# Inverse roots of layer 1's norms by GpSimd's power operation instead of Newton steps on VectorE

## The chip, the cores and the metric

The kernel runs on one core of one Trainium2 chip. The metric is the device time of one execution in microseconds (us), median of several runs. Beside it stands the profile of one execution, whose span (first to last instruction) is 1.7 to 2.2 us shorter than the time of that same execution. A run counts as slow when it is over 1.5% above the fastest of the same kernel, and as fast otherwise. The ratios below use fast runs alone, and the traces are of fast runs unless it is said otherwise; a median from a slow chip can include slow runs. The runs fell on several chips; on some of them, called slow chips below, the unchanged kernel itself takes 565 us or more instead of 504, so each kernel is compared with the runs of the unchanged kernel made with it on the same chip, and the ratios that come of this are set beside one another only where the unchanged kernel took 503 to 506 us.

## The reference, cut to what matters

Two layers work on 2708 nodes of 128 features with a sparse adjacency matrix, each followed by a residual norm. The change touches only the two norms of layer 1:

```python
def _layernorm(x, axis=-1, eps=1e-5):
    m = jnp.mean(x, axis=axis, keepdims=True)
    v = jnp.var(x, axis=axis, keepdims=True)
    return (x - m) / jnp.sqrt(v + eps)

# layer 1, for every pair (i, j) with an edge: gelu(s[i] + d[j] + msg_b), summed with weight adj
new_feats = combined @ upd_w.T + upd_b
h = gelu(new_feats) + node_feats
mu, var = mean(h), var(h)                       # per row
l1 = (h - mu) / sqrt(var + LN_EPS) * ln_w + ln_b
x = _layernorm(x + l1)
```

So each row needs two inverse square roots, one per norm, with a product by `ln_w`, a sum with `ln_b` and a sum with `x` between the two norms.

## The kernel before

The 2708 rows are 22 blocks of 128, worked through in seven groups of 4, 4, 4, 4, 3, 2 and 1 blocks. For each group GpSimd gathers rows of a table (98 gathers in all), TensorE, VectorE and ScalarE turn them into messages and sums, and `finish` makes the two norms and stores the group.

```python
GROUPS = [(0, 4), (4, 4), (8, 4), (12, 4), (16, 3), (19, 2), (21, 1)]
for g0, gn in GROUPS:
    h = fin.tile([P, gn, D], F32, name="h")
    for b in range(g0, g0 + gn):
        ...                                     # cut
        for k0 in range(t0, t1, 4):
            dd = edge.tile([P, 4, D], F32, name="dd", bufs=4)
            ...                                 # cut: w gathers, matmuls, products
                gather(dd[:, k, :], table, J[:, t : t + 1])
    finish(h, g0, gn)

def rsqrt(o, v, shape):
    h = fin.tile([P, shape], I32, name="rh")
    t = fin.tile([P, shape], F32, name="rt")
    nc.vector.tensor_scalar(h, v.bitcast(I32), 1, None, op0=OP.arith_shift_right)
    nc.vector.tensor_scalar(o.bitcast(I32), h, -1.0, MAGIC, op0=OP.mult, op1=OP.add)
    for _ in range(3):
        nc.vector.tensor_mul(t, o, o)
        nc.vector.tensor_mul(t, t, v)
        nc.vector.tensor_scalar(t, t, -0.5, 1.5, op0=OP.mult, op1=OP.add)
        nc.vector.tensor_mul(o, o, t)

def layer_norm(o, v, n):
    ...                                         # cut: tiles st, mv, ve, rs
    for k in range(n):
        nc.vector.bn_stats(st[:, k, :], v[:, k, :])
        nc.vector.bn_aggr(mv[:, k, :], st[:, k, :])
    nc.vector.tensor_scalar_add(ve, mv[:, :, 1], LN_EPS)
    rsqrt(rs, ve, n)
    for k in range(n):
        nc.vector.tensor_scalar(o[:, k, :], v[:, k, :], mv[:, k, 0:1], rs[:, k : k + 1],
                                op0=OP.subtract, op1=OP.mult)

def finish(h, b0, n):
    own = x1[:, b0 : b0 + n, :]
    v = fin.tile([P, n, D], F32, name="v")
    nc.scalar.activation(h, h, AF.Gelu)
    nc.vector.tensor_add(h, h, own)
    layer_norm(v, h, n)
    nc.gpsimd.tensor_mul(v, v, rowvec["lw"]...)   # these three are called a trio below
    nc.gpsimd.tensor_add(v, v, rowvec["lb"]...)
    nc.gpsimd.tensor_add(v, v, own)
    layer_norm(h, v, n)
    ...                                         # cut: the stores of the group's rows
```

A root is thus 2 + 3 x 4 = 14 instructions on VectorE, on `n` numbers per partition.

Of the kernel before, what the change touches and what calls it, by code (L numbers as in the profile page):

```python
# [10 lines left out]
F32 = mybir.dt.float32  # L11
U32 = mybir.dt.uint32
BF16 = mybir.dt.bfloat16
I32 = mybir.dt.int32
AF = mybir.ActivationFunctionType
OP = mybir.AluOpType
AX = mybir.AxisListType

P = 128
# [4 lines left out]
MAGIC = 1597463007.0  # L24
# [26 lines left out]
def hyperbolic_then_message_kernel(  # L51
# [16 lines left out]
    nc = tc.nc  # L68
# [11 lines left out]
    const = ctx.enter_context(tc.tile_pool(name="const", bufs=1))  # L80
# [24 lines left out]
    for name, src in (("ub", upd_b), ("lw", ln_w), ("lb", ln_b), ("mbr", msg_b)):  # L105
        t = const.tile([P, D], F32, name=name)
# [3 lines left out]
    ones = const.tile([P, P], F32, name="ones")  # L110
    nc.gpsimd.memset(ones, 1.0)

    tri = const.tile([P, P], F32, name="tri")
    nc.gpsimd.affine_select(
        tri, ones, pattern=[[1, P]], compare_op=OP.is_gt, fill=0.0, base=0, channel_multiplier=-1
# [61 lines left out]
    def cols():  # L177
        count[0] += 1
        return sc.tile([P, NB], F32, name=f"c{count[0]}")
# [55 lines left out]
    def bank(name, bufs=2):  # L235
        return ps.tile([P, 512], F32, name=name, bufs=bufs)

    with tc.tile_pool(name="stream", bufs=2) as stream, tc.tile_pool(name="small", bufs=2) as small:
# [22 lines left out]
        u, v, gam, gm1 = cols(), cols(), cols(), cols()  # L261
# [85 lines left out]
        for b in range(NB):  # L347
# [8 lines left out]
            op = bank("mp")  # L356
# [72 lines left out]
    with tc.tile_pool(name="edge", bufs=2) as edge, tc.tile_pool(name="fin", bufs=2) as fin:  # L429
# [3 lines left out]

        def rsqrt(o, v, shape):

            h = fin.tile([P, shape], I32, name="rh")
            t = fin.tile([P, shape], F32, name="rt")
            nc.vector.tensor_scalar(h, v.bitcast(I32), 1, None, op0=OP.arith_shift_right)
            nc.vector.tensor_scalar(o.bitcast(I32), h, -1.0, MAGIC, op0=OP.mult, op1=OP.add)
            for _ in range(3):  # L440
                nc.vector.tensor_mul(t, o, o)
                nc.vector.tensor_mul(t, t, v)
                nc.vector.tensor_scalar(t, t, -0.5, 1.5, op0=OP.mult, op1=OP.add)
                nc.vector.tensor_mul(o, o, t)

        def layer_norm(o, v, n):
            st = fin.tile([P, n, 6], F32, name="st1")
            mv = fin.tile([P, n, 2], F32, name="mv1")
            ve = fin.tile([P, n], F32, name="ve1")
            rs = fin.tile([P, n], F32, name="rs1")  # L450
# [6 lines that stand above are left out]
                nc.vector.tensor_scalar(  # L457
                    o[:, k, :], v[:, k, :], mv[:, k, 0:1], rs[:, k : k + 1], op0=OP.subtract, op1=OP.mult
                )
# [24 lines left out]
# [3 lines that stand above are left out]
# [6 lines left out]
                for k0 in range(t0, t1, 4):  # L493
# [4 lines left out]
                    for k in range(w):  # L498
                        t = k0 + k
# [49 lines left out]
    with tc.If(dense > 0):  # L549
        with tc.tile_pool(name="dn", bufs=1) as fin:  # L550
# [17 lines left out]
            for b in range(NB):  # L568
                h = fin.tile([P, 1, D], F32, name="h")
# [63 lines left out]
```

## Time and profile before

| | before |
|---|---|
| time, median (lowest to highest) | 503.59 us (503.42 to 503.71) |
| span of the profiled run (its own time: 504.96 us) | 503.2 us |
| VectorE (DVE) busy | 315.3 us, 63% |
| GpSimd (POOL) busy | 227.9 us, 45% |
| first gather of layer 1's table | 312.75 us |
| 98th and last gather | 444.15 us |
| last VectorE instruction ends | 498.06 us |
| last GpSimd instruction ends | 494.27 us |

The page's section on the chain of work that ended last gives, for the kernel before, its shares of the span by engine:

```profile
PE 43%; DVE 22%; POOL 15%; issue 8%; ACT 7%; DMA 5%; POOLq 0%; ACTq 0%; DVEq 0%; SPq 0%
```

VectorE's 22% and GpSimd's 15% are what a change of this kind can move; TensorE's (PE) 43% belong mostly to layer 0. The strips, the gathers and the timelines that the argument rests on are shown in the prediction.

### The profile page before, as it was taken

Reading aid. Unit: us, or ns where it says so; the run is one execution under the profiler, and the core shown is the slowest. Engines: PE = TensorE matmul, PEld = TensorE weight load, DVE = VectorE, ACT = ScalarE, POOL = GpSimd, SP = SyncE. Lnnn points to the kernel's source line nnn. Section 1 sums busy time; section 2 is a strip of 40 time slices with the busy share of each in tenths; the row PEclk is TensorE's granted clock in tenths of the full one; section 3 lists DMA queues with packets and bytes.
Section 4 is the critical chain, followed back from the end, with each engine's and each line's share of the span. In section 5 each row is a group of like instructions: output and inputs, shape, how many; then the busy total and the mean of one; then the engine's idle time right before and its main releaser. Section 6 shows DMA issues by size and latency. Waiting matters only on the chain.

```text
span 503.2 us, 7459 instructions
## 1 busy us (share of the span) xinstructions
PE 320.8 (64%) x2506; PEld 297.9 (59%) x2506; DVE 315.3 (63%) x1161; ACT 158.2 (31%) x321; POOL 227.9 (45%) x306
## 2 busy tenths in 40 slices
PE   2682998999999999994000097576777094855200
PEld 1451997999999999993000065465666094844200
DVE  3539485777676676678989965222363184755774
ACT  2953143453644544532242045211121021211100
POOL 4200077777645544542000001777777878662211
PEclk9995897999999999998555579579899679686555
DMA  7500332455464564500000012121212121210000
GB/s 262 240 1 2 115 123 110 150 198 191 157 231 144 204 222 162 195 2 0 1 0 0 1 52 65 53 53 52 52 54 53 37 74 38 68 26 23 21 18 14
DMA packets 17719, 43.55 MB, mean 87 GB/s; under 512 B 6180, under 2 KB 12620, under 8 KB 14860
## 3 DMA queue, kind: packets, MB, share of 16 engines
q1 hardware_dynamic: 10108, 35.94, 19.7%
q0 software_dynamic: 6272, 6.49, 5.5%
q10 hardware_dynamic: 1296, 0.60, 0.5%
q8 instruction: 21, 0.34, 0.3%
q14 instruction: 22, 0.18, 0.1%
HBM read 40.18 MB, written 2.83 MB: 85 GB/s over the span
## 4 chain that ended last, share of the span: by engine, by line
PE 43%; DVE 22%; POOL 15%; issue 8%; ACT 7%; DMA 5%; POOLq 0%; ACTq 0%; DVEq 0%; SPq 0%
PE mp L358 21%; POOL dd L162 10%; PE sel L334 5%; PE kx L285 5%; DMA dd<-table_dram,J 3%; PE kx L418 3%; ACT sgn L351 2%; PE ag L511 2%; DVE c L196 2%; PE kx L248 2%; DMA x_sb<-in_x_dram 2%; POOL v L475 1%; POOL v L476 1%; POOL v L477 1%; PE kx L501 1%
## 5 line engine op out<-in xcount | busy, mean ns | idle before, releaser
L162 POOL DMA_INDIRECT dd<-table_dram,J x98 | 93.9, 958 | 96.9 <-DMA table_dram<-nom 66.4
L162 POOL DMA_INDIRECT V<-in_adj_dram,F x98 | 94.5, 965 | 93.3 <-DVE F L343 57.5
L358 PE MATMUL mp<-y,aT 128*128 128x130 f32 x968 | 134.1, 286 | 3.4 <-ACT sgn L351 3.4
L358 PEld LDWEIGHTS mp<-y,aT 128*128 128x128 f32 x968 | 120.0, 196 | 3.7 <-ACT sgn L351 3.7
L290 DVE MAX8 top<-kx 128x8 f32<-128x512 f32 (+4 forms) x179 | 85.6, 512 | 6.6 <-PE kx L285 6.3
L351 ACT ACTIVATE sgn<-aT 128x2816 bf16<-128x2816 f32 x22 | 56.1, 2552 | 67.0 <-PE kx L285 56.4
L285 PE MATMUL kx<-kd,sgn 128*128 128x128 bf16 x484 | 44.8, 225 | 9.5 <-DVE top L290 9.5
L502 PE MATMUL kx<-ident,R 128*128 128x128 f32 x98 | 27.0, 322 | 32.0 <-DVE dd L508 23.6
L501 PE MATMUL kx<-y,R 128*128 128x128 f32 x196 | 39.6, 315 | 7.1 <-DVE dd L508 6.3
L508 DVE TENSOR_TENSOR dd<-kx,dd 128x512 f32<-128x512 f32 (+3 forms) x30 | 17.7, 589 | 41.3 <-DMA dd<-table_dram,J 35.2
L285 PEld LDWEIGHTS <-sgn 128*128 128x128 bf16 x484 | 36.4, 103 | 11.8 <-DVE top L290 9.2
L509 ACT ACTIVATE ge<-dd 128x512 f32<-128x512 f32 (+3 forms) x30 | 16.6, 552 | 77.2 <-DVE dd L508 43.5
L511 PE MATMUL ag<-rw,ge 128*128 128x128 f32 x196 | 35.6, 334 | 7.4 <-ACT ge L509 3.2
L501 PEld LDWEIGHTS kx<-y,R 128*128 128x128 f32 x196 | 33.7, 228 | 8.8 <-DVE dd L508 7.7
L415 PE MATMUL mp<-ident,x_sb 128*128 128x128 f32 x22 | 5.1, 317 | 50.3 <-DVE x_sb L411 50.3
L511 PEld LDWEIGHTS ag<-rw,ge 128*128 128x128 f32 x196 | 31.5, 241 | 9.3 <-ACT ge L509 8.8
L502 PEld LDWEIGHTS kx<-ident,R 128*128 128x128 f32 x98 | 15.2, 167 | 34.3 <-DVE dd L508 25.4
L415 PEld LDWEIGHTS mp<-ident,x_sb 128*128 128x128 f32 x22 | 3.5, 161 | 52.0 <-DVE x_sb L411 50.5
L334 PE MATMUL sel<-z,R 128*128 128x49 f32 (+3 forms) x196 | 28.0, 288 | 7.3 <-DVE R L309 4.5
L334 PEld LDWEIGHTS sel<-z,R 128*128 128x128 f32 x196 | 25.3, 201 | 8.9 <-issue 5.0
L452 DVE BATCH_NORM_STATS2 st<-v 128x6 f32<-128x128 f32 x22 | 5.5, 275 | 37.1 <-POOL v L477 37.1
L319 DVE TENSOR_TENSOR_SCAN scan<-m,oe 128x48 f32<-128x48 f32 (+3 forms) x24 | 8.8, 368 | 30.1 <-ACT oe L303 30.0
(169 smaller groups left out, 539.2 us busy)
## 6 DMA issues: line engine op xcount, KB each, us to landing
aT<-in_adj_t_dram SPq DMA_DIRECT2D x22, 1408.0 KB
V<-in_adj_dram,F POOLq DMA_INDIRECT x98, 2.9
dd<-table_dram,J POOLq DMA_INDIRECT x98, 2.6
table_dram<-nom SPq DMA_DIRECT2D x22, 64.0 KB
out_dram<-h SPq DMA_DIRECT2D x21, 64.0 KB
mw<-in_L_gnn_msg_w_dram ACTq DMA_DIRECT2D x1, 128.0 KB
uw<-in_L_gnn_upd_w_dram ACTq DMA_DIRECT2D x1, 128.0 KB
w_sb<-in_L_gnn_W_dram ACTq DMA_DIRECT2D x1, 64.0 KB
```

The lines of the kernel that those rows point to most:

```text
L162: nc.gpsimd.indirect_dma_start(out=o, out_offset=None, in_=src, in_offset=bass.IndirectOffsetOnAxis(ap=at, axis=0))
L285: nc.tensor.matmul(kp[:, i * P : (i + 1) * P], lhsT=sgn[:, j, :], rhs=kd[:, j, :], start=True, stop=True)
L290: nc.vector.max(top[:, c : c + 8], seg[:, s, :])
L334: nc.tensor.matmul(sp[:, k, :], lhsT=R[:, t0 + k0 + k, :], rhs=z, start=True, stop=True)
L351: nc.scalar.activation(sgn, aT, AF.Sign, accum_out=signs[:, b : b + 1])
L358: nc.tensor.matmul(op[:, : D + 2], lhsT=aT[:, j, :], rhs=y[:, j, :], start=(j == 0), stop=(j == NB - 1))
L418: nc.tensor.matmul(dp[:, : 2 * D], lhsT=x1T[:, b * P : (b + 1) * P], rhs=wT[:, 0:2, :].rearrange("p a d -> p (a d)"), start=True, stop=True,)
L501: nc.tensor.matmul(X[:, k, :], lhsT=R[:, t, :], rhs=s_nm[:, b, :], start=True, stop=True)
L502: nc.tensor.transpose(RT[:, k, :], R[:, t, :], ident)
L508: nc.vector.tensor_tensor(dd[:, :w, :], X[:, :w, :], dd[:, :w, :], op=OP.add)
L509: nc.scalar.activation(ge[:, :w, :], dd[:, :w, :], AF.Gelu)
L511: nc.tensor.matmul(ag[:, :P], lhsT=ge[:, k, :], rhs=rw[:, k, :], start=False, stop=(k0 + k == t1 - 1))
```

## The change

The intent is to take 196 short, dependent instructions off VectorE, and to replace each chain of 14 by one instruction on GpSimd, which raises the variance to the power -0.5. The diff is complete:

```diff
@@ -110,6 +110,8 @@
     ones = const.tile([P, P], F32, name="ones")
     nc.gpsimd.memset(ones, 1.0)
 
+    nhalf = const.tile([P, 1], F32, name="nhalf")
+    nc.gpsimd.memset(nhalf, -0.5)
     tri = const.tile([P, P], F32, name="tri")
@@ -433,15 +435,7 @@
         def rsqrt(o, v, shape):
 
-            h = fin.tile([P, shape], I32, name="rh")
-            t = fin.tile([P, shape], F32, name="rt")
-            nc.vector.tensor_scalar(h, v.bitcast(I32), 1, None, op0=OP.arith_shift_right)
-            nc.vector.tensor_scalar(o.bitcast(I32), h, -1.0, MAGIC, op0=OP.mult, op1=OP.add)
-            for _ in range(3):
-                nc.vector.tensor_mul(t, o, o)
-                nc.vector.tensor_mul(t, t, v)
-                nc.vector.tensor_scalar(t, t, -0.5, 1.5, op0=OP.mult, op1=OP.add)
-                nc.vector.tensor_mul(o, o, t)
+            nc.gpsimd.tensor_tensor(o, v, nhalf[:, 0:1].to_broadcast([P, shape]), op=OP.pow)
```

## The prediction

> **What bounds the kernel now.** I read the chain that ended last first, then the timeline of GpSimd and of VectorE from the first gather of the table on, because the change touches layer 1 alone. Everything ahead of it stands in the same order on every engine in both programs, so what can move is the stretch from 312.75 us to the end at 503.2 us.
>
> The page, two busy strips (tenths in 40 slices of 12.6 us) and two groups:
>
> ```profile
> DVE  3539485777676676678989965222363184755774
> POOL 4200077777645544542000001777777878662211
> ...
> L162 POOL DMA_INDIRECT dd<-table_dram,J x98 | 93.9, 958 | 96.9 <-DMA table_dram<-nom 66.4
> ...
> L452 DVE BATCH_NORM_STATS2 st<-v 128x6 f32<-128x128 f32 x22 | 5.5, 275 | 37.1 <-POOL v L477 37.1
> ```
>
> GpSimd (POOL) issues 98 gathers of 0.96 us. They start every 1.25 us (0.94 and 0.30 of issue) from 312.75 to 445.1 without a real gap: up to there GpSimd is the bound. VectorE (DVE) waits for GpSimd's three elementwise operations of a norm, 37.1 us in all.
>
> The timeline of GpSimd around the last gather:
>
> ```profile
> 444.15 0.94 POOL L162 DMA_INDIRECT dd<-table_dram,J  x1 [0.30 <-ACT ge L509]
> 445.11 1.27 POOL L475 TENSOR_TENSOR v<-v,lw 128x512 f32<-128x512 f32 x1
> 446.46 1.26 POOL L476 TENSOR_TENSOR v<-v,lb 128x512 f32<-128x512 f32 x1
> 447.80 1.26 POOL L477 TENSOR_TENSOR v<-v,x_sb 128x512 f32<-128x512 f32 x1
> 462.01 1.27 POOL L475 TENSOR_TENSOR v<-v,lw 128x512 f32<-128x512 f32 x1 [12.95 <-DVE v L457]
> ...
> 474.55 1.00 POOL L475 TENSOR_TENSOR v<-v,lw 128x384 f32<-128x384 f32 x1 [8.59 <-DVE v L457]
> ...
> 484.21 0.72 POOL L475 TENSOR_TENSOR v<-v,lw 128x256 f32<-128x256 f32 x1 [6.53 <-DVE v L457]
> ...
> 492.75 0.45 POOL L475 TENSOR_TENSOR v<-v,lw 128x128 f32<-128x128 f32 x1 [6.22 <-DVE v L457]
> ```
>
> Such three operations, a trio, stand between the two norms of each of seven groups of rows. After the last gather only the third is due; four more follow one another at intervals of 12.5, 9.7 and 8.5 us, each time waiting for VectorE. So the last 53 us are a chain between VectorE and GpSimd, and Newton steps lie in it. Its last link, on VectorE's timeline:
>
> ```profile
> 494.30 0.29 DVE L452 BATCH_NORM_STATS2 st<-v 128x6 f32<-128x128 f32 x1 [1.63 <-POOL v L477]
> 494.63 0.18 DVE L453 BATCH_NORM_AGGREGATE mv<-st 128x2 f32<-128x6 f32 x1
> 494.85 0.15 DVE L454 TENSOR_SCALAR ve<-mv 128x1 f32<-128x1 f32 x1
> 495.04 0.15 DVE L438 TENSOR_SCALAR rh<-ve 128x1 int32<-128x1 int32 x1
> 495.22 0.15 DVE L439 TENSOR_SCALAR rs<-rh 128x1 int32<-128x1 int32 x1
> ...
> 497.72 0.34 DVE L457 TENSOR_SCALAR h<-v,mv,rs 128x128 f32<-128x128 f32 x1
> ```
>
> One root takes 14 dependent instructions on a single number per partition: 495.04 to 497.72, 2.68 us, one per 0.19 us.
>
> **What the Trainium skill says.** "GPSIMD Engine Reference", 3.1 Elementwise, calls VectorE some two times faster at a two-input operation (ratio 1.96 at 2048 elements). The trace agrees: 1.27 us here for 128x512 on GpSimd against 0.68 us for the 128x512 add of L473, 1.9 times. It gives no time for a power, and no other page I found does. "Perfetto Trace Analysis", GPSIMD Engine Instruction, advises timing GpSimd by start-to-start spacing; here 1.35 us (445.11 to 446.46) against 1.27 reported, so I add 0.07. "VectorE: DVE Perf Modes", The TRN2 errata, puts a fixed cost on each VectorE instruction from SBUF: 0.15 us for one element a partition agrees, and it is why Newton on so little data is nearly all overhead.
>
> **The change, part by part.** *Removed:* 14 roots (7 groups, 2 norms) of 14 instructions, 196 on VectorE. Those of width 4 (8 roots) sum to 18.1 us in the groups by form; the 84 others at some 0.157 us to 13.2; in all 31 us of busy time. During the gathers VectorE has idle time, so most of it is worth nothing there; in the tail it is on the path.
>
> *Added:* 14 powers on GpSimd, 128x4 to 128x1, and one memset at the start. Nothing in the trace times a power. What bounds it from below is GpSimd's small operations: 0.20 us for the 128x1 copies of L326, and from 453 ns at 128 columns and 1272 at 512 a fixed part of 0.18 us with 2.1 ns a column. I choose **p = 0.6 us**, three small operations[...]; it is a choice, and the widest doubt here.
>
> *Moved:* the built program's order is changed too. Before, GpSimd runs 67 gathers ahead of the first trio; after, 56 gathers, a power, two gathers, then the first trio, split up by gathers. In VectorE's queue the normalisation stands right behind the variance, so it blocks VectorE until the power comes. The first variance was ready at 372.0 in the trace, but the 56th gather ends at some 383: an 11 us stall. It should cost GpSimd nothing: the gathers of those 11 us have their buffers. And three trios now lie before the last gather instead of two, with the fourth right behind it.
>
> I then walked all queues from 312.75 by hand rules: each instruction starts when the one before it on its engine has let go and its inputs are there, with the durations of the trace's rows, 3.2 us from a gather's start to its landing (336.10 to 339.38), and 0.18 us per TensorE pass, chosen to fit. The walk of before gives the trios at 396.8, 420.9, 444.8, 461.4, 473.6, 483.1, 491.5 and the last normalisation's end at 497.1; the trace has 397.0, 421.1, 445.1, 462.0, 474.6, 484.2, 492.8 and 498.06. So walk against walk is good to about 1 us. The walk of after with p = 0.6:
>
> - To the fourth trio: 312.75 + 98 x 1.25 (122.5) + 3 trios x 4.05 (12.15) + 7 powers x 0.67 (4.7) + waits for VectorE of 3.4 = 455.5, against 461.4: **5.9 us earlier**.
> - From the fourth trio to the end: 12.1 + 7.2 + 7.1 + 3.4 = 29.8 against 35.7: **5.9 us less**. The last term by hand: trio 1.55, statistics and variance 0.74, power with its two handovers 0.75, normalisation 0.34 = 3.4; before 5.31, of which Newton 2.68.
>
> Sum 11.8 us: 503.6 - 11.8 = **491.8 us**. The end of the kernel after the last normalisation (5.1 us, the last store) doesn't change.
>
> The same walk with other p ends 15.2 us earlier for 0.3, 7.0 for 1.0 and 0.6 for 1.5. So twelve of the fourteen powers count in full: gain = 19 - 12p. It is 10 us (2%) at p = 0.75 and nothing at p = 1.6.
>
> **The rivals.** *The power is slow.* GpSimd is the engine of the gathers, and its work there is paid at once: seven powers delay the gathers, five more lie in the tail. At p = 2 the kernel loses 5 us, at 4 us some 30. For it: GpSimd is the slower engine in the trace, and a power is dearer than a product. Against: only 1 to 4 columns. *VectorE's stall spreads.* Its 11 us block at the first root holds the adds that free gather buffers; if a gather waits, the loss is up to 11 us and the time about 500. Against: the walk finds no such wait, as four buffers hold 16 gathers. *Newton was hidden.* If the tail hung on TensorE or on the landing of the last gathers, only the order would matter and the gain would be some 6 us, 497. Against: the waits of the trios name VectorE, 12.95, 8.59, 6.53 and 6.22 us.
>
> **Range and chances.** 485 us needs p of about 0.1 with a kind walk; 504 us is p of 1.6. I take 485 to 504 for 8 in 10. Faster by over 2% needs p under 0.75: 0.56. Within 2%, p up to 2.4: 0.29. Slower: 0.15.
>
> **What would show it.** The row of the power on GpSimd: its mean decides; by 12 us for each us. VectorE idle for some 11 us before its first normalisation, with GpSimd as releaser, and gathers still at 1.25 us around it. The 98th gather at about 454. The four last trios at about 455.5, 467.6, 474.8 and 481.9, with waits ahead of them of a few us or less. It would be wrong if a power cost over 1 us, if starting the first power costs some us once, or if gathers slow down beside it.

## The result, and the profile after

The changed kernel is correct and takes 498.61 us (median of 4 runs, 497.68 to 499.33); the kernel before took 503.65 us in the same rounds (503.42 to 503.82). The ratio is 0.9899, 95% interval 0.9879 to 0.9919: some 5 us less, within 2%, where 11.8 us less had been forecast. A ratio here is the mean time of one kernel's fast runs over the mean of the other's fast runs of the same rounds, so it is not quite the ratio of the medians that are quoted.

From the page after come the two strips (tenths of busy time in 40 slices of 12.4 us), the chain's shares by engine, and the gathers' group:

```profile
DVE  2629486676867767767989983422240537545751
POOL 3200077778556354343000000677777878787441
...
PE 41%; POOL 18%; DVE 18%; issue 8%; ACT 6%; DMA 5%; ACTq 1%; POOLq 0%; DVEq 0%
...
L164 POOL DMA_INDIRECT dd<-table_dram,J x98 | 94.9, 968 | 94.8 <-DMA table_dram<-nom 66.4
```

Against before, VectorE's share of the chain fell from 22 to 18% and GpSimd's rose from 15 to 18%. The gathers cost the same (968 against 958 ns). GpSimd's busy time rose from 227.9 to 242.0 us.

The groups after, VectorE's statistics of the second norm and its two normalisations (columns: count, busy us, mean ns, idle us before and what ended it):

```profile
L446 DVE BATCH_NORM_STATS2 st<-v 128x6 f32<-128x128 f32 x22 | 5.5, 275 | 16.6 <-POOL v L471 16.6
...
L451 DVE TENSOR_SCALAR v<-h,mv,rs 128x128 f32<-128x128 f32 x22 | 6.7, 362 | 16.8 <-POOL rs L438 16.8
L451 DVE TENSOR_SCALAR h<-v,mv,rs 128x128 f32<-128x128 f32 x22 | 6.6, 355 | 17.1 <-POOL rs L438 17.1
```

VectorE's wait for the trios fell from 37.1 to 16.6 us, and 33.9 us of waiting for the powers (`rs`) came instead. A total of waits cannot tell which of it is on the path; the timelines can. First the power itself, in the groups of GpSimd after, kept apart by width:

```profile
L438 POOL TENSOR_TENSOR rs<-ve,nhalf 128x4 f32<-128x4 f32 x8 | 8.4, 1047 | 3.9 <-DVE ve L448 3.8
...
L438 POOL TENSOR_TENSOR rs<-ve,nhalf 128x3 f32<-128x3 f32 x2 | 1.7, 854 | 4.7 <-DVE ve L448 3.3 <-DVE mv L447 1.4
L438 POOL TENSOR_TENSOR rs<-ve,nhalf 128x2 f32<-128x2 f32 x2 | 1.4, 701 | 2.1 <-DVE tot L538 1.1 <-DVE ve L448 1.0
L438 POOL TENSOR_TENSOR rs<-ve,nhalf 128x1 f32<-128x1 f32 x2 | 1.1, 552 | 3.1 <-DVE ve L448 3.1
```

One power takes 1047, 854, 701 and 552 ns for four to one columns, so about 0.39 us and 0.165 us more for each column. The fourteen sum to 12.6 us, 0.90 us on average. The prediction's choice was 0.6.

The timeline of GpSimd after (start, duration, engine, line, operation; in brackets the idle time before and what ended it), around its first power and in the tail:

```profile
383.98 0.94 POOL L164 DMA_INDIRECT dd<-table_dram,J  x1 [0.30 <-issue]
384.94 1.07 POOL L438 TENSOR_TENSOR rs<-ve,nhalf 128x4 f32<-128x4 f32 x1
386.19 1.02 POOL L164 DMA_INDIRECT dd<-table_dram,J  x1 [0.18 <-issue]
387.52 0.95 POOL L164 DMA_INDIRECT dd<-table_dram,J  x1 [0.30 <-issue]
388.49 1.29 POOL L469 TENSOR_TENSOR v<-v,lw 128x512 f32<-128x512 f32 x1
...
457.33 1.08 POOL L164 DMA_INDIRECT dd<-table_dram,J  x1 [0.19 <-issue]
458.53 1.27 POOL L469 TENSOR_TENSOR v<-v,lw 128x512 f32<-128x512 f32 x1
...
470.60 1.00 POOL L469 TENSOR_TENSOR v<-v,lw 128x384 f32<-128x384 f32 x1 [0.97 <-DVE v L451]
...
478.57 0.72 POOL L469 TENSOR_TENSOR v<-v,lw 128x256 f32<-128x256 f32 x1 [0.72 <-DVE v L451]
...
485.94 0.45 POOL L469 TENSOR_TENSOR v<-v,lw 128x128 f32<-128x128 f32 x1 [0.46 <-DVE v L451]
...
488.27 0.55 POOL L438 TENSOR_TENSOR rs<-ve,nhalf 128x1 f32<-128x1 f32 x1 [0.81 <-DVE ve L448]
```

The gathers around the first power run on at 1.25 us; the last four trios start at 458.5, 470.6, 478.6 and 485.9 us, and the waits of the last three are under 1 us, against 8.59, 6.53 and 6.22 us before; the powers between them, left out here but for the last, wait 0.8 to 3.3 us each. And the last line is new: before, the last thing that GpSimd did was the seventh trio. Now it is the last power.

VectorE after, at the first normalisation:

```profile
386.05 1.19 DVE L451 TENSOR_SCALAR v<-h,mv,rs 128x128 f32<-128x128 f32 x4 [12.30 <-POOL rs L438]
```

VectorE stood still for 12.30 us there, as foreseen, and the gathers above show that GpSimd lost nothing by it.

Put side by side (times from the span's start; all are starts, except the two rows that say "ends"):

| | before | after | moved by |
|---|---|---|---|
| first gather | 312.75 | 314.05 | +1.30 |
| fourth trio | 462.01 | 458.53 | -3.48 |
| fifth trio | 474.55 | 470.60 | -3.95 |
| sixth trio | 484.21 | 478.57 | -5.64 |
| seventh trio | 492.75 | 485.94 | -6.81 |
| VectorE's last instruction ends | 498.06 | 489.21 | -8.85 |
| GpSimd's last instruction ends | 494.27 | 488.82 | -5.45 |
| end of the span | 503.2 | 497.6 | -5.6 |

VectorE finishes 8.85 us earlier and the kernel ends only 5.6 us earlier. So 3.3 us are lost after the last VectorE instruction: 5.1 us from there to the end before, 8.4 us after. What lies there shows when the line that closes the program is asked for its instructions. Among them are some named DRAIN, on every engine, called drains below; the page's "busy" time leaves them out (columns: shortest, median and longest in ns, first and last start). Before:

```profile
L620 POOLq DRAIN  x3: 40/107/7427, 494.9 to 502.9; - x3
L620 SPq DRAIN  x3: 7/7/13, 501.6 to 502.6; - x3
```

After:

```profile
L614 POOLq DRAIN  x3: 40/107/7427, 489.4 to 497.4; - x3
L614 SPq DRAIN  x3: 7/7/13, 492.6 to 497.1; - x3
```

GpSimd has three drains at the end, and the first of them takes 7.43 us (the view cut to 494.0 to 495.5 us shows it alone). It starts 0.6 us after GpSimd's own last instruction (494.27 to 494.9, 488.82 to 489.4), the last 8.0 us after it, and then the kernel is over. SyncE's first drain, which comes after the last store, starts 3.4 to 3.5 us after VectorE's last instruction (498.06 to 501.6, 489.21 to 492.6); after the change it stands 4.8 us ahead of GpSimd's last drain. The reading is a rule for this kernel: **the program ends some 8.9 us after GpSimd's last instruction or some 4.2 us after VectorE's last, whichever is later** (the 4.2 was put down before the experiments that measure it; those below give 4.2 and 4.3). Before, the first gives 494.27 + 8.9 = 503.2 and the second 498.06 + 4.2 = 502.3, so the last Newton root, the last normalisation and the store lay hidden beside the drain. After, the last power keeps GpSimd in use to 488.82, and 488.82 + 8.9 = 497.7. The rest of this document tests that rule, and the price of the power.

### The profile page after: what moved, and what is told of

Same layout as the page of the kernel before. It is cut to its first block, busy times and chain, and to the rows that moved or that the text cites. A ratio compares the mean times of both kernels' runs of the same rounds, so it can differ in the third digit from the quotient of the medians.

```text
span 497.6 us, 7268 instructions
## 1 busy us (share of the span) xinstructions
PE 322.7 (65%) x2506; PEld 298.9 (60%) x2506; DVE 298.5 (60%) x965; ACT 157.9 (32%) x321; POOL 242.0 (49%) x321
## 4 chain that ended last, share of the span: by engine, by line
PE 41%; POOL 18%; DVE 18%; issue 8%; ACT 6%; DMA 5%; ACTq 1%; POOLq 0%; DVEq 0%
PE mp L360 22%; POOL dd L164 12%; PE sel L336 5%; PE kx L287 5%; DMA dd<-table_dram,J 4%; PE kx L420 3%; POOL rs L438 2%; ACT sgn L353 2%; DVE c L198 2%; PE kx L250 2%; POOL v L469 1%; POOL v L470 1%; DVE y L196 1%; DVE top L292 1%; PE sel L304 1%
## 5 line engine op out<-in xcount | busy, mean ns | idle before, releaser
L164 POOL DMA_INDIRECT dd<-table_dram,J x98 | 94.9, 968 | 94.8 <-DMA table_dram<-nom 66.4
L164 POOL DMA_INDIRECT V<-in_adj_dram,F x98 | 94.8, 967 | 93.6 <-DVE F L345 57.7
L287 PEld LDWEIGHTS <-sgn 128*128 128x128 bf16 x484 | 36.4, 103 | 11.8 <-DVE top L292 9.2
L503 ACT ACTIVATE ge<-dd 128x512 f32<-128x512 f32 (+3 forms) x30 | 16.6, 552 | 79.9 <-DVE dd L502 64.9
L496 PE MATMUL kx<-ident,R 128*128 128x128 f32 x98 | 25.7, 323 | 22.8 <-DVE rw L498 15.0
L458 PE MATMUL sel<-wT,xT 128*128 128x128 f32 x44 | 11.3, 351 | 19.0 <-DVE h L460 19.0
```

The costliest lines, as they stand in the source:

```text
L164: nc.gpsimd.indirect_dma_start(out=o, out_offset=None, in_=src, in_offset=bass.IndirectOffsetOnAxis(ap=at, axis=0))
L287: nc.tensor.matmul(kp[:, i * P : (i + 1) * P], lhsT=sgn[:, j, :], rhs=kd[:, j, :], start=True, stop=True)
L496: nc.tensor.transpose(RT[:, k, :], R[:, t, :], ident)
L503: nc.scalar.activation(ge[:, :w, :], dd[:, :w, :], AF.Gelu)
```

## The experiments

**The theories.** The working theory (A in the expectations) is: the loss against the forecast is the power's real time, paid nearly one for one, plus the end rule above. Its rivals are B, that the moved order and not the power's time is what costs; C, that the end comes at a fixed time after VectorE's last instruction; and D, that every root moved is worth the same. Two further letters, F and G, belong to the later start of the first gather.

### A product in the power's place

Same order on every engine, a wrong result on purpose:

```diff
-            nc.gpsimd.tensor_tensor(o, v, nhalf[:, 0:1].to_broadcast([P, shape]), op=OP.pow)
+            nc.gpsimd.tensor_tensor(o, v, nhalf[:, 0:1].to_broadcast([P, shape]), op=OP.mult)
```

> The changed kernel with the power replaced by a product of the same two tiles (results wrong on purpose); the order of instructions on every engine is unchanged, so only the duration of 14 GpSimd instructions differs. Theory A (the power's own time was mis-sized, and some 12 of 14 powers count in full): the product of 128x4 takes about 0.2 us instead of 1.05, the last VectorE instruction ends about 7.6 us earlier (at some 481.5 us), and the time is about 491 us, 2.5% below the kernel before. Theory B (the new order, with VectorE's 12.3 us stall at its first root, is what eats the gain): the power's duration hardly counts, the time stays within 2 us of the changed kernel's 498.6.

Measured: 489.89 us (489.32 to 490.42), ratio to before 0.9707 (0.968 to 0.9735); wrong result, as meant. In its groups by form the operation takes 0.2 us:

```profile
L438 POOL TENSOR_TENSOR rs<-ve,nhalf 128x4 f32<-128x4 f32 x8 | 1.7, 208 | 3.8 <-DVE ve L448 3.7
```

The fourteen operations sum to 2.8 us here (8 x 0.208 and 6 x about 0.19) against 12.6 for the powers: 9.8 us less work on GpSimd. The ratios differ by 0.0192, which is 9.7 us of 504. In the traces the time from the first gather to VectorE's last instruction falls from 175.16 us to 165.83, by 9.3 us; the expectation had 7.6. What the powers cost beyond a cheap operation is paid nearly in full, and rival B is out.

### Each power twice

```diff
+            t = fin.tile([P, shape], F32, name="rt")
+            nc.gpsimd.tensor_tensor(t, v, nhalf[:, 0:1].to_broadcast([P, shape]), op=OP.pow)
             nc.gpsimd.tensor_tensor(o, v, nhalf[:, 0:1].to_broadcast([P, shape]), op=OP.pow)
```

> The changed kernel with every power computed twice, the first into a scratch tile; results right, order otherwise unchanged. Theory A: each further power costs its own 1.05 us (4 columns) to 0.55 us (1 column); by hand walk the last VectorE instruction moves 11.2 us later, time about 510 us, slower than the kernel before by over 1%. Theory B (the order): under 3 us more than the changed kernel.

Measured: 512.33 us, ratio 1.0138 (1.0108 to 1.0169), so 0.0239 or 12.0 us above the changed kernel, for some 12.3 us of further powers on GpSimd (8.1 + 1.7 + 1.4 + 1.1). In the trace VectorE's last instruction ends at 500.73 us, 11.5 us later than in the changed kernel (11.2 expected), or 11.7 counted from the first gather: again nearly one for one. Most of the 2 us above the expected 510 lies after the work. GpSimd's last power ends at 500.34, and its drain begins 2.1 us after that instead of 0.6:

```profile
L616 POOLq DRAIN  x3: 40/107/7427, 502.5 to 510.5; - x3
```

The span ends 10.4 us after the last power, where the rule has 8.9. Why the drain begins later here is not shown.

### Only the last root back to Newton steps

The changed kernel, whose last root alone is made on VectorE again (`newton` is the old `rsqrt`):

```diff
-            layer_norm(h, v, n)
+            layer_norm(h, v, n, newton if b0 == 21 else rsqrt)
```

> The changed kernel with only the very last root (second norm of the last group, one column) done by Newton steps on VectorE again. Theory A (the end is GpSimd's last instruction plus its drain, 8.9 us in both traces, or VectorE's last plus some 4.2 us, whichever is later): VectorE's last instruction ends 2.3 us later (about 491.5), but GpSimd's last is now the trio at about 487.5, so the span is about 496.4, some 1.2 us SHORTER than the changed kernel although the chain is longer. Theory C (the end is a fixed time after VectorE's last instruction, 8.4 us in the changed program): 2.3 us longer than the changed kernel, about 500.9 us of time.

Measured: 497.58 us, ratio 0.9862 (0.9835 to 0.9888); the changed kernel's was 0.9899, with intervals that overlap, so the time alone only says that it got no slower: the 0.9945 of the rival lies outside. In the trace VectorE ends at 490.76, which is 1.55 us later than in the changed kernel, and the span is 495.9, which is 1.7 us shorter. The spans of all runs of the two kernels, which fell in different rounds, average 496.8 and 495.9, which is 0.9 us of difference and not 1.7. A longer chain on VectorE with an earlier end is what the rule says and what no fixed end allows: GpSimd is done at 486.95 (the seventh trio), and 486.95 + 8.9 = 495.9.

### The kernel before, with the last group's trio on VectorE

```diff
+            eng = nc.vector if b0 == 21 else nc.gpsimd
-            nc.gpsimd.tensor_mul(v, v, ...)     # and the two sums
+            eng.tensor_mul(v, v, ...)
```

> The kernel before, Newton everywhere, with only the last group's three elementwise operations moved from GpSimd to VectorE; order otherwise unchanged. Theory A: GpSimd's last instruction ends at about 486.5 instead of 494.3, its drain is then hidden, and the span ends some 4.2 us after VectorE's last instruction, which comes 0.6 us earlier: 1.5 us less than the kernel before. Theory C (a fixed 5.1 us after VectorE's last instruction): only 0.6 us less.

Measured: 503.87 us against 504.46 for before on that chip, ratio 0.9981 (0.9969 to 0.9994); by time alone it cannot tell the two expectations apart. In the trace the span is 501.5 us, GpSimd is done 15.2 us before the end and VectorE, which ends at 497.22, 4.3 us before it:

```profile
L621 POOLq DRAIN  x3: 40/107/7427, 486.7 to 501.2; - x3
L621 SPq DRAIN  x3: 7/7/13, 500.6 to 500.9; - x3
```

GpSimd's long drain begins at 486.7 and is over by 494.1; it has the same length where nothing waits for it. Here VectorE's last normalisation and its store decide, not the drain.

### A late touch of GpSimd

The kernel before, with one small copy on GpSimd after the last normalisation, which nothing waits for. It was run three times, under three labels, because each time it fell on a chip where every kernel takes some 570 us.

```diff
             layer_norm(h, v, n)
+            if b0 == 21:
+                late = fin.tile([P, 1], F32, name="late")
+                nc.gpsimd.tensor_copy(late, h[:, 0, 0:1])
```

> The kernel before with one copy of 128x1 on GpSimd into a scratch tile added, reading the last group's normalised rows, so that GpSimd's last instruction comes after VectorE's last; nothing else moves. Theory A (the end is GpSimd's last instruction plus 8.9 us, of which 7.43 us are its drain): GpSimd ends at about 498.3 instead of 494.3, the span grows by about 4.0 us, time +0.8%. Theory C (the end is a fixed time after VectorE's last instruction): no change, within 0.5 us.

> The kernel before, with one small GpSimd copy of the last normalised value after the last normalisation; nothing waits for the copy. Theory A (GpSimd closes the program with a drain of 7.43 us after its own last instruction, so work of VectorE beside the drain is hidden and work before it is not): GpSimd's last instruction ends at about 498.3 instead of 494.3, the span grows by about 4.0 us, ratio to before 1.008. Theory C (the end depends on the last normalisation and its store alone): no change, ratio 1.000. A first run of it fell on a chip where all kernels are 70 us slower and decided nothing.

> Third try of the kernel before with one small GpSimd copy after the last normalisation, in the hope of a chip on which the kernel before takes some 504 us. Theory A (GpSimd's drain follows its own last instruction and is on the path from then on): GpSimd's last instruction moves from about 494.3 to 498.3, span and time grow by about 4.0 us, ratio 1.008. Theory C (the end follows the last normalisation and its store alone): ratio 1.000.

Measured, ratios to before: 1.0035 (0.9994 to 1.0077), 1.0134 (1.006 to 1.0209) and 1.0086 (1.0031 to 1.0141). On kernels of 570 us the rule's 4.0 us are 1.007, which lies in all three intervals; 1.000 lies in the first only. In the third run's trace the last normalisation ends at 566.95 us, the copy at 567.19, and the span 9.2 us after the copy and 9.45 after the normalisation. Without the copy it was 5.1 us after the normalisation, on the fast chip and also on this one (562.41 and 567.5, in a kernel that differs from the one before by an unused constant). One copy of 0.18 us, on an idle engine, for a value that nobody reads, makes the kernel longer.

### Early powers, late powers

The powers in the first three groups only, and in the last four groups only, with Newton steps elsewhere. Both fell first on a slow chip and were repeated.

```diff
-            layer_norm(v, h, n)                 # and the second norm alike
+            layer_norm(v, h, n, newton if b0 >= 12 else rsqrt)     # early powers
+            layer_norm(v, h, n, rsqrt if b0 >= 12 else newton)     # late powers
```

> Powers on GpSimd for the first three groups only (six roots), Newton steps on VectorE in the last four. Theory A (the power pays in the last stretch alone; during the gathers six powers delay GpSimd, which is the bound there, and the removed Newton steps lay in VectorE's idle time): by hand walk 2.5 us longer than the kernel before, about 506 to 507 us. Rival D (each root moved is worth the same, 6 of 14 of the measured 5.0 us): 2.2 us shorter than the kernel before.

> Newton steps on VectorE in the first three groups, powers on GpSimd in the last four (eight roots). Theory A: by hand walk the last GpSimd instruction ends 0.7 us earlier than in the changed kernel, so the time is about 0.5 to 1 us below the changed kernel's, near 498: all the gain and a little more from 8 of 14 powers. Rival D: 8 of 14 of 5.0 us, that is 2.9 us shorter than the kernel before, near 501.

> The same kernel as the earlier run with powers in the first three groups only; that run fell on a chip where the kernel before itself took 573 us, with waits in places that the first chip does not show, so it is repeated. Expectation unchanged: theory A 2.5 us longer than the kernel before; rival D (each root worth the same) 2.2 us shorter.

> The same kernel as the earlier run with powers in the last four groups only, repeated for the same reason. Theory A: 5.5 to 6 us shorter than the kernel before (0.5 to 1 us better than all fourteen powers); rival D: 2.9 us shorter.

Measured on the slow chip (before: 572.81 us): 0.9897 (0.984 to 0.9953) and 0.9886 (0.9854 to 0.9918). There the first gather starts at 354.58 and 351.65 us, and the gathers wait 21.8 and 31.4 us for ScalarE's results, a wait of 1.9 to 3.8 us in the traces of the fast chips, so these two say nothing of the 504 us kernel. Measured on a fast one: early powers 505.65 against 505.68 us, ratio 0.9996 (0.9978 to 1.0014), which neither expectation had: the powers among the gathers neither gain nor lose. Late powers 502.57 us, ratio 0.992 (0.9891 to 0.9949), 4 us less; this lies between the two expectations and decides neither. The gain of the change thus comes from the last four groups. With early powers the third trio starts at 439.45 instead of 445.11, and yet the fourth starts at 463.49 instead of 462.01, after 6.09 us of waiting for VectorE: the lead is lost again before the tail. No run takes the Newton steps away without the moved order, so how much of the gain is due to each is not shown.

### All trios on VectorE

First the kernel before with its trios moved, then the changed kernel with its trios moved:

```diff
-            nc.gpsimd.tensor_mul(v, v, ...)     # and the two sums
+            nc.vector.tensor_mul(v, v, ...)
```

> Newton steps on VectorE as before, but the three elementwise operations of every norm moved from GpSimd to VectorE. If GpSimd's queue is the bound through the gathers and the chain between VectorE and GpSimd sets the last stretch, this takes 8 us off GpSimd before the last gather and shortens each link after it: by hand walk VectorE's last instruction comes 11.2 us earlier, and with GpSimd's drain hidden behind it the span is about 12 us shorter, near 491.5 us of time, better than the changed kernel by 7. If VectorE becomes the bound instead, it stays above 498.

> The changed kernel with the three elementwise operations of every norm moved from GpSimd to VectorE, all roots powers on GpSimd. By hand walk GpSimd's last instruction, the last power, ends 12 us earlier than in the changed kernel (476.6 against 488.8), and with its 8.9 us to the end the span is about 485.5: 17 to 18 us shorter than the kernel before on a chip like the first.

Measured: the first fell on the slow chip, 0.9915 (0.9871 to 0.9959), its profile in the slow state, and is no basis for anything. The second: 489.45 us (488.52 to 490.16), ratio 0.9671 (0.9652 to 0.9689), correct, 3.3% faster than before.

### The version that follows from the rule

The changed kernel with the trios on VectorE, Newton steps in the first two groups (where VectorE has time and GpSimd has none), powers from the third group on, and Newton steps again for the last root:

```diff
-            layer_norm(v, h, n)
-            nc.gpsimd.tensor_mul(v, v, ...)     # and the two sums
-            layer_norm(h, v, n)
+            layer_norm(v, h, n, newton if b0 < 8 else rsqrt)
+            nc.vector.tensor_mul(v, v, ...)
+            layer_norm(h, v, n, newton if b0 == 21 or b0 < 8 else rsqrt)
```

> The elementwise operations on VectorE for every group; powers on GpSimd from the third group on, Newton steps on VectorE for the first two groups and for the very last root, so that fewer powers delay the gathers and GpSimd's drain starts before the last root. By hand walk VectorE's last instruction ends at 477.4 and GpSimd's last at 472; the span is VectorE's end plus 4.2, about 481.6: 21 us shorter than the kernel before, and 3 to 4 us better than the run with all roots as powers.

Measured: 484.93 us (482.91 to 486.49), ratio 0.9582 (0.9544 to 0.9621), correct: the fastest of all, 4.2% under the kernel before. It and the version ahead of it ran on the same chip, and are the cleanest test of the rule, since VectorE ends at the same time in both. They differ in two things, the first two groups and the last root, which were not tried apart. With powers to the end (the timeline of all engines, then the drains at the end of the program):

```profile
476.95 0.55 POOL L438 TENSOR_TENSOR rs<-ve,nhalf 128x1 f32<-128x1 f32 x1 [2.24 <-DVE ve L448]
477.54 0.34 DVE L451 TENSOR_SCALAR h<-v,mv,rs 128x128 f32<-128x128 f32 x1 [0.73 <-POOL rs L438]
```

```profile
L615 POOLq DRAIN  x3: 40/107/7427, 478.1 to 486.1; - x3
```

With Newton steps for the last root, the same two views (the first line stands for two powers):

```profile
471.33 1.22 POOL L438 TENSOR_TENSOR rs<-ve,nhalf 128x2 f32<-128x2 f32 x2 [3.51 <-DVE ve L460]
...
477.37 0.35 DVE L463 TENSOR_SCALAR h<-v,mv,rs 128x128 f32<-128x128 f32 x1
```

```profile
L626 POOLq DRAIN  x3: 40/107/7427, 472.7 to 481.7; - x3
L626 SPq DRAIN  x3: 7/7/13, 481.1 to 481.4; - x3
```

VectorE ends at 477.88 in one and 477.72 in the other; the spans are 486.3 and 481.9. The ratios differ by 0.0089, or 4.5 us of the 505.68 us that before took there, with intervals that don't meet. The drain of the second begins at 472.7, early enough that SyncE's drain (481.1, 3.4 us after VectorE) comes last. So the gain over the version ahead of it lies after VectorE's last instruction.

### The last group without late GpSimd work, and the later start

Four kernels were sent together for what was still open; the third late touch and a second try of the constant followed. All fell on slow chips. Two concern the end or the start in the changed kernel, two the start in the kernel before. The changed kernel with the last group's trio on VectorE and its last root in Newton steps:

```diff
+            eng = nc.vector if b0 == 21 else nc.gpsimd
-            layer_norm(h, v, n)
+            layer_norm(h, v, n, newton if b0 == 21 else rsqrt)
```

> The changed kernel with the last group's three elementwise operations on VectorE and its last root in Newton steps, so GpSimd's last instruction is the last group's first power and all that follows is VectorE's. Theory A (end = the later of GpSimd's last instruction plus 8.9 us and VectorE's last plus 4.2 us): the end after VectorE's last instruction falls from 8.4 to about 4.2 to 5 us; VectorE's own chain is about as long as the changed kernel's, so the time is about 2.5 to 3.5 us less than the changed kernel's, ratio to before 0.984. Theory C (the end is a fixed time after VectorE's last instruction): no shorter than the changed kernel, ratio 0.990 or more.

Measured: 551.14 us against 566.39 (medians with slow runs in them; the ratio is of fast ones), ratio 0.9747 (0.9657 to 0.9837). Compared with the changed kernel proper this means nothing, as it was run on another chip. In the trace the end comes 4.3 us after VectorE's last instruction (543.88, span 548.2), and in the next kernel, which ends in a power, on the same chip 8.4 us (536.14, span 544.5). That is the rule again.

The constant `nhalf` made later in the program, in the changed kernel, and the constant alone, unused, in the kernel before (twice):

```diff
+    nhalf = sc.tile([P, 1], F32, name="nhalf")         # changed kernel: after the tile nom
+    nc.gpsimd.memset(nhalf, -0.5)
```

> The changed kernel with the constant allocated and set later in the program instead of among the first constants. Theory F: the first gather is back near 312.75 and the kernel about 1.1 us faster than the changed one, ratio to before 0.9877. Theory G: first gather where the changed kernel has it or anywhere within 312.4 to 314.1, ratio 0.990.

> The kernel before with the unused constant and its memset only. Theory F (the constant itself delays the start, by its place in memory or its memset): the first gather comes at about 313.9 instead of 312.75 and the time is 1.0 us longer, ratio 1.002. Theory G (the later start has to do with something else, or is scatter between loads of a program): first gather within 0.4 us of 312.75, ratio 1.000.

> Second try of the kernel before with the unused constant and its memset only. Theory F (the constant delays the start): first gather at about 313.9 instead of 312.75, 1.0 us longer, ratio 1.002. Theory G (scatter between loads of a program, or something else of the changed kernel): first gather within 0.4 us of 312.75, ratio 1.000.

Measured: 0.9769 (0.968 to 0.9858) for the first, not comparable with another chip's 0.9899; 1.003 (0.9995 to 1.0065) and 0.9973 (0.992 to 1.0025) for the constant alone. Theory F wanted 1.002 and G 1.000, and these intervals hold one or both: by time undecided. The first gathers on these chips lie between 344.96 and 356.01 us with or without the constant, too widely for a question of 1 us. On the fast chips all kernels with the constant began at 313.2 to 314.1 us and the two without it at 312.4 and 312.75.

The start of the traces says more, because the chips differ little there. Before and after, TensorE's first instruction:

```profile
8.58 0.66 PE L245 MATMUL mp<-ident,x_sb 128*128 128x128 f32 x2 [8.58 <-DMA x_sb<-in_x_dram]
```

```profile
9.34 0.66 PE L247 MATMUL mp<-ident,x_sb 128*128 128x128 f32 x2 [9.34 <-DMA x_sb<-in_x_dram]
```

It waits for the loads of the node features `x_sb`, the first of which is issued at 0.87 to 0.88 us in every trace. In the six traces without the constant it starts at 8.19 to 8.79 us; in the thirteen with the constant among the first ones at 9.17 to 9.55, and the two with the unused constant alone are among these (9.55 and 9.29); with the constant made later it starts at 8.28. So the constant in that place does delay the start, as theory F has it, by 0.76 us here of the 1.30 at the first gather. Why the load takes longer, and where the other 0.5 us arise, stays open.

### The end rule in the traces of the fast chips

| kernel | VectorE's last ends | GpSimd's last ends | span | after VectorE | after GpSimd |
|---|---|---|---|---|---|
| before | 498.06 | 494.27 | 503.2 | 5.1 | **8.9** |
| changed | 489.21 | 488.82 | 497.6 | 8.4 | **8.8** |
| a product in the power's place | 479.27 | 478.88 | 488.1 | 8.8 | **9.2** |
| each power twice | 500.73 | 500.34 | 510.7 | 10.0 | **10.4** |
| last root back to Newton | 490.76 | 486.95 | 495.9 | 5.1 | **8.95** |
| before, last trio on VectorE | 497.22 | 486.28 | 501.5 | **4.3** | 15.2 |
| early powers | 498.23 | 494.42 | 503.3 | 5.1 | **8.9** |
| late powers | 491.97 | 491.58 | 500.4 | 8.4 | **8.8** |
| trios on VectorE, powers | 477.88 | 477.50 | 486.3 | 8.4 | **8.8** |
| the version of the rule | 477.72 | 472.55 | 481.9 | **4.2** | 9.35 |

The bold number is the one that the rule names as the limit. Where VectorE's chain and its store are last, it is 4.2 to 4.3. Where GpSimd is last it is 8.8 to 8.95 in six traces, but 9.2 with the product, as with the late copy on the slow chips, and 10.4 with each power twice. There the drain begins 0.9 and 2.1 us after GpSimd's last instruction instead of 0.6. So the 8.9 is 7.43 us of drain, some 0.9 us after it, and a gap ahead of it that is not the same in every program.

## Why the prediction was wrong

It was wrong in size: 491.8 us forecast, 498.6 measured; the measured time lay within the stated range of 485 to 504. Two of its steps failed: the price of a power, p = 0.6 us, which measured 0.90 us, and the end of the kernel, held fixed at 5.1 us, which became 8.4.

*What held.* VectorE's block at the first root was 12.30 us (11 forecast) and cost the gathers nothing. The gathers' idle time did not grow (96.9 us before, 94.8 after), so the rival that the stall spreads is out. The rival that Newton was hidden behind TensorE or the last gathers is out as well, as the tail did get shorter by 5.4 us; but the last root was hidden, by something that no rival named (term 2). The waits of the last three trios for VectorE fell to under 1 us each, with waits of 0.8 to 3.3 us ahead of the powers of the tail in exchange. From the fourth trio to VectorE's last instruction the time fell from 36.05 to 30.68 us; 5.9 less was forecast, 29.8 long.

*Term 1, the price of the power.* "I choose p = 0.6 us" was the step marked as the widest doubt, and it failed: the mean was 0.90 us, 1.05 at four columns, where "over 1 us" was one of the prediction's own signs of being wrong. In the prediction's own formula, 19 - 12p, this makes a gain of 8.2 us instead of 11.8, that is 3.6 less. The product in its place and the doubled power show that the price is paid nearly one for one: 9.33 us in the traces for a mean power cheaper by 0.70 us, 11.67 for one dearer by 0.88, so 13.3 us for each us of p rather than 12. With this term right and nothing else, the forecast would have been 495.4 us, 1.6% under before; so this step alone takes the forecast from over 2% to under it. The rival "the power is slow" was the right one, in a mild form.

*Term 2, the end.* "The end of the kernel after the last normalisation (5.1 us, the last store) doesn't change" failed: it went from 5.1 to 8.4 us, 3.3 us of gain lost. The 5.1 us was no property of the store. It was what was left of GpSimd's drain, counted from another engine's last instruction. The prediction subtracted Newton's 2.68 us from the last link as if they were on the path; the rule shows that they were beside the drain, and that the last power lengthened what was on it. Putting that one root back shortened the span by 1.7 us in the trace.

*Term 3, the start.* The first gather came 1.30 us later than before, which no step of the prediction foresaw ("Everything ahead of it stands in the same order"). 0.76 us of it are there at TensorE's first instruction and come with the new constant; the cause of the rest is open.

*What the walk left out in the other direction.* From the first gather to VectorE's last instruction the time fell from 185.31 to 175.16 us, 10.15 us less, where the formula with the real p gives 8.2: it was 2 us too low. The kernel with the product shows the same sign: 165.83 us from its first gather (313.44) to VectorE's last instruction (479.27), 19.5 us less than before, where the formula with p = 0.2 gives 16.6. So the hand walk was good to 2 or 3 us, not to about 1, and its error partly made up for the terms that failed; that was luck. (One reading in it is off by little: 1.35 against 1.27 us is 0.08 for each power, where 0.07 was added.)

The sum: 11.8 - 3.6 + 2.0 - 1.3 - 3.3 = 5.6 us, which is the difference of the spans (503.2 - 497.6). The 2.0 is what is left over, so that the sum closes is no test. The times differ by 5.0 us.

The two terms that failed on size were both things that the trace of before could not show, or showed in a view that was not read. The power's time stood in no row of it. GpSimd's drain did: it was there in the instructions of the line that closes the program, and it was not asked for, because the page names "busy" work only and a drain is none.

## What to carry to other kernels

Ask what each engine does after its last real instruction, before any time is taken off the last link of a chain: the end may be set by another engine's close-down, and then work in the last link is free and a small late instruction on the wrong engine is not. Measure an operation that stands in no row before its price is multiplied by fourteen; here its row in the trace after gave the price, and one kernel with another operation in its place and one with it doubled showed that some 95% of it was paid. And put a chain of small operations where the engine has time in that stage: Newton steps early, powers in the tail and Newton again for the last root was better than powers everywhere (0.9582 against 0.9671, with the trios on VectorE in both), though in the traces nearly all of that difference lies after VectorE's last instruction, so what the early Newton steps gave is not shown. Newton steps everywhere with the trios on VectorE were measured on a slow chip alone, so that comparison is missing.

## What the Trainium skill lacked or had wrong

- "GPSIMD Engine Reference" and every other page searched: no time for a power on GpSimd. The runs show 552, 701, 854 and 1047 ns for one to four columns on 128 partitions, float32, against 190 to 208 ns for a product in its place. What section 3.1 Elementwise says of ordinary two-input operations gives no hint of this.
- "VectorE: DVE Perf Modes", The DRAIN you can't avoid, says of the drains that the runtime puts around a program that they take about 12 ns each, on all five engines. The drains here belong to a line of the program, the one that closes it, so they do not contradict the page, but it does not name them. Those of VectorE (10 to 17 ns), ScalarE and TensorE (8 ns) and SyncE (7 to 13 ns) are of that size; GpSimd's take 40, 107 and 7427 ns in every fast trace here, with the long one in the time that is measured.
- No page found says that this long drain follows GpSimd's own last instruction and so makes late GpSimd work cost more than it lasts: 8.8 to 8.95 us from that instruction to the end in six of the traces above where it decides, 9.2 and 10.4 in two, against 4.2 to 4.3 us from VectorE's last instruction. "Runtime: NRT & Kernel Launch", The ~15µs preamble/postamble breakdown, lists the runtime's own stages around a kernel, and has no row of this size.
